# An exchange through DRAM whose four writes are cut by destination and not by source partitions

## The chip, the cores and the metric

The kernel runs on one core of a Trainium2 chip. The metric is the device time of one execution in microseconds (us), as the median of three runs; lower is better. The engines are TensorE (PE, matrix products), VectorE (DVE), ScalarE (ACT), GpSimd (POOL) and SyncE (SP, which issues transfers). SyncE, ScalarE and GpSimd each have a queue of transfers of their own (q1, q10 and q0 in the profile), and the core has 16 DMA engines that carry them out.

## The reference

There are two layers over 8 sequences of 128 tokens with 512 features, all in float32, and each adds its result to the stream. The first applies a chosen 512 x 512 matrix for each sequence and a linear layer with a low-rank mixture of two of eight experts. The second is the one around the change: attention with 32 query heads and 8 key and value heads of width 128, over a paged cache of 512 positions and the sequence's own 128 positions, and then a gated low-rank feed-forward network (16 of 64 experts).

```python
q = rope(rmsnorm(x @ Wq.T)); k = rope(rmsnorm(x @ Wk.T)); v = x @ Wv.T
k_all, v_all = concat(cache[block_table], own)     # 512 + 128 positions
scores = where(valid, q @ k_all.T * SCALE, -1e30)
o = softmax(scores) @ v_all
x = x + ffn(o @ Wo.T)
```

The valid positions of the cache come from the lengths that are given for each sequence, and those positions are below the length. Four query heads share one key and value head.

## The kernel before, in words

**The work is cut into 64 units.** A unit is one sequence and one key head with its four query heads; two units (two key heads) make a step, and four groups of two heads pass over the 8 sequences. The units run as a software pipeline that is written out by hand: every engine's order is the program's order, with no scheduler in between (`tc.manual_schedule`, L87). `iteration(u)` (L1264) computes in one pass the scores and the softmax of unit u, the product with the values of unit u - 2, the output projection of unit u - 3 and the projections and the rotary embedding of units ahead. The function runs for u from 1 to 66 (L1397); unit 0 is done beside the first layer (L732 to L828).

**The softmax of a unit.** For each of the four heads, TensorE computes 128 x 640 scores (`scores`, L434: L439 against the cache, L442 against the sequence's own keys), VectorE adds the mask and scales (`mask_exp`, L447, L452), ScalarE takes the exponential (L463), and GpSimd divides by the sum (`normalize`, L466, L469).

**The exchange.** The product with the values needs the probabilities transposed: positions on the partitions, where the softmax left tokens. The kernel does not use TensorE for that. VectorE turns the 32 x 32 blocks (`blocks`, L471, the transpose of L474), which leaves every block at its old place; moving the blocks between the partitions is done by a write to DRAM and a read back. The buffer `pb` has 128 partitions, and on each there are four stretches of 800 numbers: stretch k holds what has to get to the partitions 32 k to 32 k + 31. Of the 800, 640 are probabilities of four heads, and 160 (the rotated queries and the key of unit u + 2, turned by `blocks_qk`, L423, the transpose of L425) ride along. The units 62 and 63 have no such passengers and write 640.

- `exchange_out(u)` (L479) writes `pb` to a DRAM tile `px` of shape 4 x 32 x 4 x 800: (destination k, row b within the destination's partitions, source i, stretch). It issues four writes, two on SyncE's queue and two on ScalarE's (L486). Write i takes the partitions 32 i to 32 i + 31 with all their four stretches.
- `exchange_in(u)` (L930), called a pass later, reads it back on SyncE's queue: `qkb` (L934), then `pT` (L937), in which partition 32 k + b has its four rows of DRAM in a line.
- `heads_qk` (L940) copies `qkb` into the operand of the next unit's scores on ScalarE (L944); `values` (L950) multiplies `pT` with the values (L957).

**What orders it.** `pb` has one buffer (L421, a pool with one buffer), so the transposes of unit u + 1 into it (first L425, and then L474 four times) wait until the writes of unit u have read it. In `iteration(u)`, SyncE first issues five loads of key pages (`gather`, L182, L193), then the two reads of the exchange of unit u - 1, then three more pages (L1286 to L1290), and at the end of the pass the writes of unit u (L1372). Each of these instructions waits in its queue's order. GpSimd issues the value rows (L203, indirect), the weights (`wqkv`, `wo`) and a part of the output (`yd`, `yp`) on its own queue.

**Beside it.** The projections use products of the Strassen-Winograd kind (L243 to L284, L1079 to L1130), with the additions spread over VectorE and GpSimd. The end of the kernel has a second, smaller exchange of the same layout (`turn_out`, L377), which the change doesn't touch.

Of the kernel before, what the change touches and what calls it, by code (L numbers as in the profile page):

```python
# [33 lines left out]
QD = P // 32  # L34
# [24 lines left out]
def adaln_ffn_kernel(  # L59
# [25 lines left out]
    nc = tc.nc  # L85
# [393 lines left out]
    def exchange_out(u):  # L479

        pb = pb_t.pop(u)
        m = dram_x.tile([QD, 32, QD, XW], F32, tag="px", name=f"px_{u}")
        w = XW if u + 2 in range(4, NU) else PW
        for i in range(QD):
            eng = nc.sync if i < QD // 2 else nc.scalar
            eng.dma_start(  # L486
                out=m[:, :, i, :w].rearrange("k b f -> b k f"),
                in_=pb[i * 32 : (i + 1) * 32, :, :w],
            )
        px_t[u] = m  # L490


    with ExitStack() as l0:
# [322 lines left out]
        blocks(0, 2)  # L816
        blocks(0, 3)
        exchange_out(0)
        l0_turn(B - 2)
        l0_experts(B - 1)  # L820
# [105 lines left out]
    with ExitStack() as l1:  # L926
# [337 lines left out]
        def iteration(u):  # L1264
# [104 lines left out]
            if on(u):  # L1369
                blocks(u, REP - 2)  # L1370
                blocks(u, REP - 1)
                exchange_out(u)  # L1372
# [186 lines left out]
```

## Time and profile before

| What | Value |
|---|---|
| time, median of 3 runs | 1204.23 us (1203.33 to 1204.79) |
| profiled execution, its own time | 1207.58 us |
| its span, first to last instruction | 1205.5 us |
| granted TensorE clock | 1.0 |
| busy: ACT, POOL, DVE | 504.9, 741.0, 913.2 us |
| transfers: bytes, mean rate | 302.31 MB, 251 GB/s |
| share of 16 DMA engines: q1 (SyncE), q0 (GpSimd) | 53.1%, 12.3% |
| exchange writes, issues on SyncE / ScalarE | 128 / 128 |
| exchange reads, pT / qkb | 64 / 60 |

How to read it: the profile is of one execution, so the sums in the text are made against its own time, and the runs lie a few microseconds beside it. Busy times are unions of an engine's instructions; instructions that only issue transfers aren't counted as busy, and they stand in the timeline under the name of the queue (SPq, ACTq). The chain of waits follows the work that ended last back from the end: at each step to what released it. A line of a DMA queue has its packets, its megabytes and the time of its packets as a share of 16 engines' time in the window. A packet is what one DMA engine moves in one go; here it is a row (3200 B for an exchange write), and after the rows there are small packets of 4 B that report the end.

### The profile page before, as it was taken

To read this page: it belongs to the slowest core of one execution; us is meant where nothing else is said; L and a number is where in the kernel's file an instruction comes from. 1 tells how busy PE (TensorE), PEld (TensorE's weight loads), DVE (VectorE), ACT (ScalarE), POOL (GpSimd) and SP (SyncE) were. 2 spreads that over 40 slices of the span, in tenths; PEclk is the share of its full clock that TensorE was granted. 3 is DMA by queue.
4 is the path that set the end of the run, shared out by engine and by line. 5 is a ranking of instruction groups with operands and counts; after the bars stand their busy time and mean duration, and the time that the engine had idled before them with its cause. 6 is when DMAs were issued, how large, how long until landed. Compare 5 with 4: busy or idle time off the path is not lost.

```text
span 1205.5 us, 16789 instructions
## 1 busy us (share of the span) xinstructions
PE 1194.1 (99%) x4156; PEld 715.1 (59%) x4156; DVE 913.2 (76%) x2103; ACT 504.9 (42%) x1457; POOL 741.0 (61%) x828
## 2 busy tenths in 40 slices
PE   9999999999999999999999999999999999999998
PEld 7766555565655556555555565555656555555554
DVE  2557788788988887878887787889887788887632
ACT  1345534444444444434444444444444444443211
POOL 3554868778756777578656685787657784643100
PEclk9999999999999999999999999999999999999999
DMA  8823777888779978888889978987889888887742
GB/s 316 305 77 118 249 247 238 261 272 289 230 252 261 323 241 268 279 274 275 254 255 283 284 228 278 294 288 254 268 256 303 247 266 249 269 277 229 234 138 97
DMA packets 205444, 302.31 MB, mean 251 GB/s; under 512 B 84771, under 2 KB 119332, under 8 KB 204324
## 3 DMA queue, kind: packets, MB, share of 16 engines
q1 hardware_dynamic: 170164, 196.29, 53.1%
q10 hardware_dynamic: 18864, 52.57, 13.7%
q0 software_dynamic: 16320, 52.40, 12.3%
q8 instruction: 33, 0.54, 0.2%
q14 instruction: 63, 0.52, 0.1%
HBM read 185.44 MB, written 115.74 MB: 250 GB/s over the span
## 4 chain that ended last, share of the span: by engine, by line
PE 83%; DMA 7%; DVE 3%; POOL 2%; SPq 2%; issue 2%; ACT 1%; ACTq 0%; DVEq 0%; POOLq 0%
PE o L957 18%; PE p L262 17%; PE s L439 16%; PE y L1082 12%; PE s L442 4%; DMA kt<-in_kc 3%; PE p L295 3%; DMA px<-pb 2%; PE cp L627 2%; PE op L1446 2%; PE bp L649 2%; PE y L1095 2%; PE fr L867 1%; SPq L192 1%; DVE pb L474 1%
## 5 line engine op out<-in xcount | busy, mean ns | idle before, releaser
L463 ACT ACTIVATE p<-p,low 128x640 f32<-128x640 f32 x256 | 211.9, 828 | 429.1 <-DVE den L468 270.1
L469 POOL TENSOR_SCALAR p<-p,den 128x640 f32<-128x640 f32 x256 | 210.9, 825 | 229.8 <-DVE den L468 228.9
L452 DVE CUSTOM_DVE_ANT_0 p<-s,mask,rs 128x640 f32<-128x640 f32 x256 | 222.4, 878 | 82.2 <-PE s L442 81.3
L262 PE MATMUL p<-wqkv,xo 128*128 128x384 f32 x784 | 281.0, 487 | 0.6 <-POOL wqkv L163 0.4
L439 PE MATMUL s<-kt,qkT 128*128 128x512 f32 x504 | 258.4, 594 | 5.3 <-DMA kt<-in_kc 4.1
L957 PE MATMUL o<-pT,vt 128*128 128x512 f32 x512 | 230.2, 592 | 0.0
L474 DVE STREAM_TRANSPOSE pb<-p 128x640 f32<-128x640 f32 x248 | 204.8, 826 | 23.4 <-POOL p L469 23.2
L1082 PE MATMUL y<-wo,oT 128*128 128x256 f32 x784 | 206.5, 380 | 0.5 <-DVE yp L1151 0.4
L262 PEld LDWEIGHTS p<-wqkv,xo 128*128 128x128 f32 x784 | 148.3, 190 | 69.8 <-POOL wqkv L163 1.4
L442 PEld LDWEIGHTS s<-qkT 128*128 128x128 f32 x504 | 95.8, 190 | 120.5 <-issue 120.5
L203 POOL DMA_INDIRECT vt<-in_vc,vrow x128 | 138.2, 1080 | 41.6 <-issue 31.9
L957 PEld LDWEIGHTS o<-pT,vt 128*128 128x128 f32 x512 | 97.2, 190 | 107.9 <-issue 92.8
L439 PEld LDWEIGHTS s<-kt,qkT 128*128 128x128 f32 x504 | 94.5, 190 | 78.3 <-issue 34.5
L1082 PEld LDWEIGHTS y<-wo,oT 128*128 128x128 f32 x784 | 131.8, 191 | 9.4 <-PE s L442 0.8
L311 ACT ACTIVATE sq<-c 128x128 f32<-128x128 f32 x320 | 98.9, 309 | 9.5 <-DVE oT L474 1.4
L442 PE MATMUL s<-qkT 128*128 128x128 f32 x504 | 96.8, 274 | 0.0
L317 POOL TENSOR_TENSOR rs<-ss,mhalf 128x5 f32<-128x5 f32 x64 | 83.8, 1310 | 5.3
L980 ACT COPY oT<-o 128x512 f32<-128x512 f32 x64 | 37.5, 586 | 106.9 <-PE o L957 79.9
L315 POOL TENSOR_SCALAR ss<-ss,eps 128x5 f32<-128x5 f32 x64 | 25.0, 391 | 76.0 <-ACT sq L311 76.0
L957 PE MATMUL o<-pT,vn 128*128 128x512 f32 x128 | 65.4, 592 | 0.0
L265 DVE TENSOR_TENSOR c<-c,p 128x384 f32<-128x384 f32 x84 | 44.9, 534 | 25.6 <-PE p L262 25.5
L425 DVE STREAM_TRANSPOSE pb<-ca 128x640 f32<-128x640 f32 x60 | 50.1, 834 | 17.2 <-DMA kt<-in_kc 11.7
(198 smaller groups left out, 1442.5 us busy)
## 6 DMA issues: line engine op xcount, KB each, us to landing
pT<-px SPq DMA_DIRECT2D x64, 1280.0 KB
px<-pb SPq DMA_DIRECT2D x120, 400.0 KB
px<-pb ACTq DMA_DIRECT2D x120, 400.0 KB
qkb<-px SPq DMA_DIRECT2D x60, 320.0 KB
kt<-in_kc SPq DMA_DIRECT2D x512, 32.0 KB
wqkv<-in_wqkv POOLq DMA_DIRECT2D x32, 384.0 KB, 4.6
wo<-in_wo POOLq DMA_DIRECT2D x17, 512.0 KB, 7.8
yd<-yp POOLq DMA_DIRECT2D x12, 512.0 KB, 9.3
```

What stands on the lines that cost most here:

```text
L203: nc.gpsimd.indirect_dma_start(out=kv_t[step][1][:, c, :], out_offset=None, in_=vc, in_offset=bass.IndirectOffsetOnAxis(ap=vrow[:, hf, at ...
L262: nc.tensor.matmul(out=ps, lhsT=xo[:, pr, x, c, :], rhs=w[:, c, :], start=(c == 0), stop=(c == 1))
L311: nc.scalar.activation(sq, cs[:, at : at + D], AF.Square, accum_out=ss[:, h : h + 1])
L317: nc.gpsimd.tensor_tensor(rs, ss, mhalf, ALU.pow)
L439: nc.tensor.matmul(out=s[:, :L], lhsT=qkT[:, h, :], rhs=kt[:, :, g % GH, :], start=True, stop=True)
L442: nc.tensor.matmul(out=s[:, L:NK], lhsT=qkT[:, h, :], rhs=qkT[:, REP, :], start=True, stop=True)
L452: nc.vector.tensor_tensor_reduce(out=p, in0=s_t.pop((u, h))[:, :NK], in1=mask_t[st], scale=rs_t[u][:, h : h + 1], scalar=BIG, op0=ALU.add, ...
L463: nc.scalar.activation(p, p, AF.Exp, bias=low, scale=-1.0, accum_out=den)
L469: nc.gpsimd.tensor_scalar(p_t[u, h], p_t[u, h], den, 1.0, ALU.mult, ALU.mult)
L474: nc.vector.transpose(pb_t[u][:, :, h * w : (h + 1) * w].rearrange("p i (j a) -> p j i a", a=32), p_t.pop((u, h)).rearrange("p (j i a) -> ...
L957: nc.tensor.matmul(out=o, lhsT=vt[:, c, j * D : (j + 1) * D] if c < LC else vn_t.pop(u), rhs=pT[:, c], start=(c == 0), stop=(c == LC),)
L1082: nc.tensor.matmul(out=y_t["y"][:, half * HN : (half + 1) * HN], lhsT=part(key)[:, i * S : (i + 1) * S], rhs=wo_t[:, slot(w, key[0] // (B ...
```

## The change

Before, write i takes 32 partitions and serves all four destinations; after it, write k takes one stretch from all 128 partitions and serves one destination. The number of writes, the queues, the bytes and the places in DRAM stay the same, and so do the two reads. In `exchange_out` (L479):

```diff
-        for i in range(QD):
-            eng = nc.sync if i < QD // 2 else nc.scalar
+        for k in range(QD):
+            eng = nc.sync if k < QD // 2 else nc.scalar
             eng.dma_start(
-                out=m[:, :, i, :w].rearrange("k b f -> b k f"),
-                in_=pb[i * 32 : (i + 1) * 32, :, :w],
+                out=m[k, :, :, :w].rearrange("b i f -> i b f"),
+                in_=pb[:, k, :w],
             )
```

As the instructions carry it, a write before goes over its target as 32 x 4 x 800 numbers and over its source as 32 x 4 x 800 (32 partitions, four stretches). After the change the target is gone over as 4 x 32 x 800 (source block i outermost, then the row b), and the source as 128 x 800. A run of 800 numbers is 3200 B in both, and there are 128 of them in each write. The orders of the instructions on TensorE, VectorE and GpSimd are the same in both kernels; on SyncE and ScalarE only these writes differ.

## Prediction

> **What bounds the kernel now.** I read the page from its chain of waits, then SyncE's timeline of one unit, then the queues and packets of the exchange. The shares and the chain:
>
> ```profile
> PE 1194.1 (99%) x4156; PEld 715.1 (59%) x4156; DVE 913.2 (76%) x2103; ACT 504.9 (42%) x1457; POOL 741.0 (61%) x828
> ...
> PE 83%; DMA 7%; DVE 3%; POOL 2%; SPq 2%; issue 2%; ACT 1%; ACTq 0%; DVEq 0%; POOLq 0%
> PE o L957 18%; PE p L262 17%; PE s L439 16%; PE y L1082 12%; PE s L442 4%; DMA kt<-in_kc 3%; PE p L295 3%; DMA px<-pb 2%; PE cp L627 2%; PE op L1446 2%; PE bp L649 2%; PE y L1095 2%; PE fr L867 1%; SPq L192 1%; DVE pb L474 1%
> ```
>
> TensorE sets the end (83% of the chain), but transfers hold 7% of it, and the exchange's writes 2% (2.4% in the chain in order of time, 29 us). So the exchange is nearly late already. One unit on SyncE's queue:
>
> ```profile
> 335.26 0.81 SPq L486 DMA_DIRECT2D px<-pb  x2
> 337.48 6.23 SPq L193 DMA_DIRECT2D kt<-in_kc  x5
> 343.89 0.54 SPq L934 DMA_DIRECT2D qkb<-px  x1
> 344.48 0.62 SPq L937 DMA_DIRECT2D pT<-px  x1
> 345.62 2.02 SPq L193 DMA_DIRECT2D kt<-in_kc  x3
> 351.67 0.81 SPq L486 DMA_DIRECT2D px<-pb  x2
> ```
>
> This is a closed loop. The read qkb waits for all four writes. The one buffer pb is refilled by the VectorE transpose of L425 (343.94 here) only once they have left it, and then come four transposes of L474 and the next four writes at 351.67: 16.4 us a turn. Over the turns in the packet records: 7.9 us (median) from the issue to the write's last packet (0.8 until the first, 7.1 of packets), then 8.5 us to the next issue, 7.0 in the shortest turn. The writes follow one another strictly; what a write lasts longer, beyond what TensorE's own work covers, lengthens every turn. From exchange 2 (issued at 142.9) to exchange 63 (1136.9) there are 61 turns.
>
> **What the change keeps.** Four writes a unit, two on SyncE and two on ScalarE; 128 rows of 3200 B each, the same bytes, places and waits. No instruction of TensorE, VectorE or GpSimd moves. Only the walk differs: the target was walked 32 x 4 x 800 and is now walked 4 x 32 x 800, while the source is 128 rows instead of 32 x 4. So two things can change: how many of the 16 DMA engines share one write, and what one packet lasts.
>
> **How many engines.** Each engine that works on a transfer ends its share with a 4-byte packet. ScalarE's queue shows it:
>
> ```profile
> q10 hardware_dynamic: 18864, 52.57, 13.7%
> ```
>
> It carried 131 transfers (128 exchange writes, one xT, two wqkv), and 131 x (128 + 16) = 18864: 128 rows and 16 small packets each. In the packet records q1 has 13618 packets of 4 B for 853 transfers: 851 x 16, plus two with one each. Those two are ids and pg, which have a single row. In the first 2.5 us q1 shows only ids, with a data packet and one small packet:
>
> ```profile
> q1 hardware_dynamic: 2, 0.00, 0.0%
> ...
> ids<-in_lora_ids SPq DMA_DIRECT2D x1, 0.0 KB
> ```
>
> So a first count of 1 uses one engine, first counts of 32 and 128 use 16. No row has 4. The bounds are 1 engine and 16; I take **4**, the reading that both rows fit: a transfer is dealt out along its first count, at most to 16. I also take it that every write gets the same four, so that 12 stand idle; no row shows which engines a smaller transfer gets, and four different fours would be the 16-engine rival again. The step to 4 is an inference from two far rows, and the largest risk here.
>
> [...]
>
> **What a packet lasts.** In windows with only this exchange, the first with SyncE's first write alone, the second with both queues' writes:
>
> ```profile
> q1 hardware_dynamic: 29, 0.09, 94.1%
> ```
> ```profile
> q1 hardware_dynamic: 47, 0.15, 53.6%
> q10 hardware_dynamic: 48, 0.15, 47.8%
> ```
>
> The last column is a share of 16 engines: 0.941 x 16 x 0.5 us / 29 = 260 ns; then 0.536 x 16 x 0.8 / 47 = 146 ns and 0.478 x 16 x 0.8 / 48 = 127 ns. Over the whole execution the 3200 B packets average 189 ns on SyncE's queue and 160 on ScalarE's, with a floor of 126. Bounds 126 and 260; I take 175, the mean of the two averages, since four engines with two queues each are neither the crowd of the first row nor surely the order of the second.
>
> [...]
>
> **The sum.** Each of the four engines gets 4 x 128 / 4 = 128 packets a unit (32 before): 128 x 0.175 = 22.4 us. Other transfers share these engines: GpSimd's queue 12.3% of 1205.5 us, 2.3 us for each of 64 units, and kt 1.1 us (8 transfers of 128 packets of 18 ns over 16 engines); 2.7 of these 3.4 fall into a window that is three quarters of the turn. 22.4 + 2.7 = 25.1 us of packets against 7.1: +18.0 a turn. The 8.5 us after a landing may shrink towards 7.0, as TensorE has run ahead by then (VectorE's own work between 343.94 and 351.67 is 6.9 us): bounds 0 to -1.5, I take -0.75. So **+17.2 us a turn**, 33.6 in all.
>
> Does that turn hold the rest? The four engines need 22.4 + 3.4 + 4.3 (reads qkb and pT: 32 packets of 32 ns and 32 of 102 each) = 30.1 of 33.6. TensorE's 16.4 us of a unit fit as well. ScalarE's and SyncE's issues (0.36 and 0.33 us each) could grow to the 0.54 of the qkb row: at most 0.4 us a turn. kt's issues queue behind the write on SyncE, where the next instruction waits for that write anyway. A long write could also hold its issuing engine; no row shows that, and I put 0 to 2 us on it and take 0.
>
> 61 x 17.2 = 1049. At the ends: exchange 2 waits on SyncE for exchange 1 (+10), and the last unit's L957 waits longer for pT: write and read take some 31 us where 21 lie between now (1136.9 to 1157.8), and I take half of the 10 as hidden behind the gate work there (+5). 1207.6 (the profiled execution; its span is 1205.5) + 1049 + 15 = 2272; the median of the runs shown lies 3.4 lower: **2268 us**.
>
> **Rivals.**
> - *Four engines, packets at the floor.* 128 x 0.126 + 2.7 = 18.8; +11.7 - 0.75 = 11.0; 61 x 11.0 + 15 gives 1890; with -1.5 about 1840. For it: with a quarter of the engines, the memory side has room. Against it: the floor held only while the two queues read different partitions.
> - *Four engines that meet.* 128 x 0.260 + 2.7 = 36.0; +28.9 - 0.75 = 28.1; 61 x 28.1 + 15 gives 2935. For it: 32 packets at 260 ns whenever one write runs alone; both queues now walk the same rows. Against it: in the second window the engines fell out of step by themselves.
> - *All 16 engines stay* (the other side). If the shares are dealt by rows, whatever their order, a write takes every partition and no packet lasts 260 ns: 32 x 0.126 + 1.1 = 5.1 us instead of 7.1. TensorE fills 99% of the span, so only what the chain holds for px is to be won: 29 us x 2.0 / 7.9 = 7, 1197 us; down to 1180 if kt's waits shorten with it. It decides only where all 16 engines take part: with 8, 64 x 0.126 + 1.1 = 9.2 us is still over 7.1.
> - *One engine.* 512 x 0.126 = 64.5 us: 61 x 59.4 + 15 gives about 4840. Only the row of ids speaks for it, and that had nothing to divide.
>
> **Chances.** Forecast (2050 to 2600) 0.50; floor (below 2050) 0.20; meeting (above 2600) 0.18; 16 engines 0.10; one engine 0.02. The range from the floor to the meeting case, 1830 to 2935, leaves out about 0.15. A measurement of this kernel can tell about 0.2% from no change. The 16-engine case is faster in 0.06, the same in 0.02, slower in 0.02; all else is slower: 0.92.
>
> **What would show it.** Right: q10 at 17328 packets (131 x 144 less 128 x 12); the DMA row near 4 tenths instead of 8, TensorE near 53%; SyncE from px to qkb 26 us, from qkb to px about 7.5; the chain mostly "DMA px<-pb", and VectorE waiting at L425. Wrong step by step: 18864 packets refute the four engines; 17328 with px to qkb near 20 or 37 us refutes the 175 ns; a much longer stretch from qkb to px shows a held engine that I left at nothing.

## The result and the profile after

The changed kernel takes 2070.57 us (median of 6 runs, 2064.45 to 2075.05) against 1203.78 us for the kernel before in the same runs: a ratio of 1.7192, with a 95% interval of 1.7158 to 1.7226. The profiled execution's span is 2072.0 us, against 1205.5. The forecast was 2268 us with a range of 1830 to 2935.

The page of the changed kernel, in its shares, its DMA row (tenths of 16 engines, in 40 slices) and its chain of waits:

```profile
PE 1365.2 (66%) x4156; PEld 786.9 (38%) x4156; DVE 911.6 (44%) x2103; ACT 503.8 (24%) x1457; POOL 736.6 (36%) x828
...
DMA  8334444444354344444435334444444444454343
...
DMA 62%; PE 11%; issue 10%; DVE 9%; POOL 4%; ACT 2%; SPq 1%; ACTq 0%; DVEq 0%; POOLq 0%
DMA px<-pb 58%; DVE pb L474 5%; POOL p L469 3%; PE o L957 2%; PE cp L627 1%; PE op L1446 1%; PE bp L649 1%; PE p L262 1%; DMA pT<-px 1%; DMA kt<-in_kc 1%; DVE yp L1151 1%; PE s L439 1%; DVE c L265 1%; PE p L295 1%; DMA px<-wo 1%
```

The chain has turned over: 83% TensorE before, now 58% one transfer, the exchange's write. At the same time the 16 DMA engines are busy in 4 tenths instead of 8. The bottleneck is DMA, and the DMA row is half empty: such a pair suggests that the work isn't spread over the engines.

The packets of ScalarE's queue say how far it is spread (packets, MB, share of 16 engines):

```profile
q10 hardware_dynamic: 17328, 52.56, 7.8%
```

That is 1536 fewer than the 18864 before: 128 writes times 12. Each write ends in 4 small packets instead of 16. The packet records agree: in 94% of the time in which rows of an exchange write are under way, there are at most four of them, from both queues together, where 16 was the commonest number before. So both queues share the same four engines. The share of 7.8% looks harmless; on four engines it is four times as much.

One turn on SyncE's queue of the changed kernel (start, duration):

```profile
701.70 1.21 SPq L486 DMA_DIRECT2D px<-pb  x2
704.29 8.33 SPq L193 DMA_DIRECT2D kt<-in_kc  x5
723.82 0.59 SPq L934 DMA_DIRECT2D qkb<-px  x1
724.46 0.61 SPq L937 DMA_DIRECT2D pT<-px  x1
725.60 2.03 SPq L193 DMA_DIRECT2D kt<-in_kc  x3
730.70 2.15 SPq L486 DMA_DIRECT2D px<-pb  x2
```

From the write's issue to the read 22.1 us, where it was 8.6; from the read to the next write 6.9, where it was 7.8. VectorE shows who waits in between. The first two lines are its timeline, the third is from the list of waits (sum in us, times, longest), and the last is that wait in the kernel before, from the list of those who waited for px (sum, times):

```profile
710.52 0.16 DVE L468 RECIPROCAL den<-den 128x1 f32<-128x1 f32 x1
723.96 0.84 DVE L425 STREAM_TRANSPOSE pb<-ca 128x640 f32<-128x640 f32 x1 [13.29 <-DMA px<-pb]
```
```profile
DVE pb L425 <- DMA px<-pb: 810.6, 58, 18.2
```
```profile
  DVE pb L425: 5.0, 6
```

The refill of pb stood 13.3 us for the write of the unit before. Over the execution this wait alone is 810.6 us (5.0 before), and the span grew by 866.5. Between exchanges 2 and 63 lie 61 turns in both traces: 993.7 us before (142.9 to 1136.6), 1836.7 after (159.6 to 1996.3). That is 843.0 of the growth; the way to exchange 2 took 16.7 longer, what follows exchange 63 took 6.8.

### The profile page after: what moved, and what is told of

The parts are those of the page before. It is cut to its first block, busy times and chain, and to the rows that moved or that the text cites. A ratio compares the mean times of both kernels' runs of the same rounds, so it can differ in the third digit from the quotient of the medians.

```text
span 2072.0 us, 16791 instructions
## 1 busy us (share of the span) xinstructions
PE 1365.2 (66%) x4156; PEld 786.9 (38%) x4156; DVE 911.6 (44%) x2103; ACT 503.8 (24%) x1457; POOL 736.6 (36%) x828
## 3 DMA queue, kind: packets, MB, share of 16 engines
q10 hardware_dynamic: 17328, 52.56, 7.8%
## 4 chain that ended last, share of the span: by engine, by line
DMA 62%; PE 11%; issue 10%; DVE 9%; POOL 4%; ACT 2%; SPq 1%; ACTq 0%; DVEq 0%; POOLq 0%
DMA px<-pb 58%; DVE pb L474 5%; POOL p L469 3%; PE o L957 2%; PE cp L627 1%; PE op L1446 1%; PE bp L649 1%; PE p L262 1%; DMA pT<-px 1%; DMA kt<-in_kc 1%; DVE yp L1151 1%; PE s L439 1%; DVE c L265 1%; PE p L295 1%; DMA px<-wo 1%
## 5 line engine op out<-in xcount | busy, mean ns | idle before, releaser
L262 PE MATMUL p<-wqkv,xo 128*128 128x384 f32 x784 | 327.7, 545 | 361.6 <-DVE c L265 354.7
L439 PE MATMUL s<-kt,qkT 128*128 128x512 f32 x504 | 306.1, 693 | 311.8 <-ACT qkT L944 285.8
L425 DVE STREAM_TRANSPOSE pb<-ca 128x640 f32<-128x640 f32 x60 | 50.7, 845 | 828.4 <-DMA px<-pb 810.6
L957 PE MATMUL o<-pT,vt 128*128 128x512 f32 x512 | 256.6, 648 | 5.1 <-DMA pT<-px 5.1
L439 PEld LDWEIGHTS s<-kt,qkT 128*128 128x128 f32 x504 | 106.9, 221 | 398.6 <-ACT qkT L944 310.6
L1082 PE MATMUL y<-wo,oT 128*128 128x256 f32 x784 | 234.7, 421 | 6.5 <-DVE yp L1151 4.6
L957 PEld LDWEIGHTS o<-pT,vt 128*128 128x128 f32 x512 | 111.8, 219 | 138.6 <-issue 130.7
L442 PEld LDWEIGHTS s<-qkT 128*128 128x128 f32 x504 | 108.5, 215 | 146.8 <-issue 146.8
L1082 PEld LDWEIGHTS y<-wo,oT 128*128 128x128 f32 x784 | 146.9, 212 | 25.6 <-PE s L442 5.3
L1151 DVE TENSOR_TENSOR yp<-yp,y 128x512 f32<-128x512 f32 (+3 forms) x94 | 59.9, 637 | 0.0
L311 ACT ACTIVATION_READ_ACCUMULATOR sq<-c 128x1 f32 x320 | 59.8, 187 | 0.0
```

What stands on the lines that cost most here:

```text
L262: nc.tensor.matmul(out=ps, lhsT=xo[:, pr, x, c, :], rhs=w[:, c, :], start=(c == 0), stop=(c == 1))
L311: nc.scalar.activation(sq, cs[:, at : at + D], AF.Square, accum_out=ss[:, h : h + 1])
L439: nc.tensor.matmul(out=s[:, :L], lhsT=qkT[:, h, :], rhs=kt[:, :, g % GH, :], start=True, stop=True)
L442: nc.tensor.matmul(out=s[:, L:NK], lhsT=qkT[:, h, :], rhs=qkT[:, REP, :], start=True, stop=True)
L957: nc.tensor.matmul(out=o, lhsT=vt[:, c, j * D : (j + 1) * D] if c < LC else vn_t.pop(u), rhs=pT[:, c], start=(c == 0), stop=(c == LC),)
L1082: nc.tensor.matmul(out=y_t["y"][:, half * HN : (half + 1) * HN], lhsT=part(key)[:, i * S : (i + 1) * S], rhs=wo_t[:, slot(w, key[0] // (B ...
```

## The experiments

In the packet records, a turn can be cut in three: from the first issue to the first packet, the time from the first to the last packet of the write, and from there to the next issue. All numbers are means over the turns 2 to 61, in us, and the packet is a row of 3200 B. The first count, of which the expectations speak, is the outermost of the counts by which a write goes over its target or its source (the smaller one, where the two differ):

```
kernel       DMA engines    turn   to first   packets   to next   ns per   time, us
             for a write            packet              issue     packet   (ratio to before)
before       16             16.28     0.88       7.08     8.32     174.6   1203.78
after         4             30.21     1.23      21.58     7.40     146.5   2070.57 (1.72)
two_counts    2             45.06     1.21      36.36     7.49     135.7   3017.72
one_queue     4             29.81     1.27      21.12     7.42     145.5   2053.33
far_rows      4             29.80     1.20      21.20     7.39     145.2   2044.47
sixteen      16             18.24     1.62       8.60     8.02     160.5   1332.89 (1.11)
rows         16             18.95     2.29       6.51    10.15     133.2   1370.95 (1.14)
crossed      16             17.22     0.96       8.59     7.67     222.7   1262.33 (1.05)
```

The kernel before ran beside each of the experiments, at medians of 1205.55 to 1206.12 us. two_counts, one_queue, far_rows, before_pool and three_one were run once, the others 4 to 10 times.

### Half the first count: two_counts

```diff
+            for i in (0, 2):
                 eng.dma_start(
-                    out=m[k, :, :, :w].rearrange("b i f -> i b f"),
-                    in_=pb[:, k, :w],
+                    out=m[k, :, i : i + 2, :w].rearrange("b i f -> i b f"),
+                    in_=pb[i * 32 : (i + 2) * 32, k, :w],
                 )
```

> Each of the four writes by destination is cut in two, so that its target is walked 2 x 32 x 800 and its source has 64 partitions; eight writes a unit, same rows, places and bytes. Theory (a write is dealt out along its first count, always over the same lowest engines): two engines get 256 packets each a unit. With the 146 ns a packet that the changed kernel shows, 256 x 0.1465 + 2.8 = 40.3 us of packets instead of 21.6; a turn of 30.2 + 18.7 = 48.9; 2071 + 61 x 18.7 = 3210 us, 2890 at the floor of 126 ns. q10 shows 256 x 66 + 432 = 17328 packets. Rival (a small transfer gets other engines each time, or the number does not come from the first count): the eight writes spread, the time is 2071 or less, and the packets on q10 are another number (17840 with four engines each).

Measured: 3017.72 us and 17328 packets on q10.

```profile
q10 hardware_dynamic: 17328, 52.56, 4.8%
```

The theory's number of packets comes out, and the time lies between its floor (2890) and its value (3210). The write's packets take 36.4 us, against 21.6 with four engines; from about the sixteenth microsecond on, 16 packets end in a microsecond (2 engines / 0.126 us = 15.9), where four engines reach 31.7. So the number of engines follows the first count, and the eight writes don't spread over others: in 95% of the time in which rows are under way, there are at most two. That all writes share the same engines was an assumption of the prediction, and this run supports it; which of the 16 they are, the records don't tell, so "lowest" in the theory is not shown. The miss within the theory is the packet: 136 ns on average instead of the 146.5 that I had carried over.

### One queue: one_queue

```diff
-            eng = nc.sync if k < QD // 2 else nc.scalar
+            eng = nc.sync
```

> The changed kernel with all four writes on SyncE's queue. Theory (the four engines' own rate bounds a write, whatever queue it comes from): 128 packets an engine as before, so 2071 within 60 us; q10 shows only 432 packets. Rival (the two queues disturb each other on the four engines, or their descriptors come late because of each other): without the second queue the slow first 4 us of each write go, about 3 us a turn, and the time falls to 1890 or so. Second rival (one queue alone can't keep four engines full): above 2200.

Measured: 2053.33 us, and on the queue of ScalarE only what it loads itself:

```profile
q10 hardware_dynamic: 432, 0.79, 0.1%
```

One queue fills the four engines as well as two do. Both rivals fall: the packets take 21.1 us instead of 21.6.

### The same cut on 16 engines: sixteen and rows

In sixteen each write by destination is split into its four sources, so that its first count is 32 again:

```diff
+            for i in range(QD):
                 eng.dma_start(
-                    out=m[k, :, :, :w].rearrange("b i f -> i b f"),
-                    in_=pb[:, k, :w],
+                    out=m[k, :, i, :w],
+                    in_=pb[i * 32 : (i + 1) * 32, k, :w],
                 )
```

> The same cut by destination and the same places, but each write is split into its four sources: 16 writes a unit of 32 partitions x 800, eight on each queue, source by source within a destination. First count 32, so 16 engines by the theory. Packets as in the kernel before (7 us of packets a unit); added are 12 issues a unit of 0.33 to 0.52 us, six on each queue (2 to 3 us until the last one is out), and a semaphore's turn comes round after eight transfers. Theory: 1204 + 61 x (1 to 5) = 1265 to 1510 us, and q10 shows 64 x 8 x 48 + 432 = 25008 packets. Rival (the order by destination itself, or where its rows fall in DRAM, costs the time): stays near 2071.

Measured: 1332.89 us, ratio 1.1081 (1.1020 to 1.1141), and 25008 packets on q10, as worked out. The order by destination and the places in DRAM are those of the changed kernel, so neither is what costs 867 us.

```profile
q10 hardware_dynamic: 25008, 52.59, 13.0%
```

What is left of the loss, 127 us, goes with the 16 issues; no run separates them from the rest. On ScalarE's timeline the eight issues stretch over 7.9 us, and its next copy stands behind them:

```profile
710.73 7.88 ACTq L487 DMA_DIRECT2D px<-pb  x8
718.65 0.59 ACT L981 COPY oT<-o 128x512 f32<-128x512 f32 x1 [7.86 <-DMA px<-pb]
```

In rows there are four writes from all 128 partitions, and the DRAM tile is laid out so that a write is one line; the reads are cut into four for it:

```diff
-        m = dram_x.tile([QD, 32, QD, XW], F32, tag="px", name=f"px_{u}")
+        m = dram_x.tile([QD, QD, 32, XW], F32, tag="px", name=f"px_{u}")
...
-                out=m[k, :, :, :w].rearrange("b i f -> i b f"),
+                out=m[k, :, :, :w].rearrange("i b f -> (i b) f"),
...
-            nc.sync.dma_start(out=pT, in_=m[:, :, :PW])
+            for k in range(QD):
+                nc.sync.dma_start(
+                    out=pT[k * 32 : (k + 1) * 32],
+                    in_=m[k, :, :, :PW].rearrange("i b f -> b i f"),
+                )
```

(and the same four reads for qkb).

> Four writes by destination, each from all 128 partitions, but the DRAM tile is laid out as destination, source, row: a write is 128 x 800 in one line on both sides. The reads pay for it: qkb and pT are read in four parts each, 32 partitions from 32 x 4 runs. Theory: 16 engines for writes (q10 back at 18864 packets) and reads; a write of all partitions takes 5 to 7 us of packets instead of 21.6; the eight reads cost six more issues of about 0.55 us on SyncE, 3.3 us a turn, partly hidden: 1190 to 1400 us. Rival (the rows' order by destination is what costs): near 2071.

Measured: 1370.95 us, ratio 1.1383 (1.1363 to 1.1403). Its queue and a turn on SyncE:

```profile
q10 hardware_dynamic: 18864, 52.57, 10.3%
```
```profile
706.04 1.79 SPq L935 DMA_DIRECT2D qkb<-px  x4
708.23 1.81 SPq L942 DMA_DIRECT2D pT<-px  x4
710.56 2.06 SPq L193 DMA_DIRECT2D kt<-in_kc  x3
714.42 4.79 SPq L486 DMA_DIRECT2D px<-pb  x2
```

18864 packets: with a first count of 128 on both sides, all 16 engines work (131 x 144 packets, 16 small ones a write). This is the cut by destination without the loss of engines. Its rows last 133 ns on average, against 175 before; the wish to read from all partitions has something to it. But the packets of a unit take only 0.6 us less (6.51 against 7.08), because SyncE's two issues now lie 4.5 us apart in this turn (4.79 us for the pair, 0.81 before; 4.35 apart on average). The list of waits of SyncE's queue shows what the second one stands for:

```profile
SPq L486 <- DMA px<-pb: 228.4, 56, 7.3
```

In the records of the instructions, the transfers of SyncE and ScalarE share eight semaphores in rotation (123 transfers on each in the kernel before), and an issue names its own semaphore as one that it waits for, that is, for the landing of the transfer that had it last. With six reads more in the rotation, SyncE's second write comes upon the semaphore of a write that ScalarE has just issued for the same exchange (58 of 62 times), so it is issued when that one has landed (here at 718.88, 0.02 us after it). The stretch from the last packet to the next issue, in which the cut reads lie, grew too, from 8.3 to 10.2 us.

### Which partitions run together: crossed

```diff
-            eng = nc.sync if i < QD // 2 else nc.scalar
+            eng = nc.sync if i % 2 == 0 else nc.scalar
```

This is an edit of the kernel before.

> The kernel before (writes by source, 16 engines) with the two queues' shares exchanged: SyncE issues sources 0 and 2, ScalarE 1 and 3, so that the two writes in flight together take partitions 0 to 31 and 32 to 63, then 64 to 95 and 96 to 127, where before they took 0 to 31 beside 64 to 95. Nothing else changes. Theory (packets last about 250 ns where the engines meet on the same quarter-pairs of partitions, 126 ns where they don't): most packets at 220 to 260 ns, 8.5 to 9.5 us of packets a unit instead of 7.1, +1.4 to 2.4 us a turn, of which some may be hidden: 1240 to 1345 us. Rival (a packet's length depends on how many transfers run, not on which partitions): mean packet within 10 ns of 175, time within 6 us of 1204.

Measured: 1262.33 us, ratio 1.0463 (1.0422 to 1.0503). The rows last 209 ns on SyncE's queue and 237 on ScalarE's (189 and 160 before), and the share of ScalarE's queue shows it at once, with the packets unchanged:

```profile
q10 hardware_dynamic: 18864, 52.57, 19.2%
```

(13.7% before.) The theory holds: 53% of the rows last 220 to 260 ns (15% before), and the packets of a unit take 8.6 us instead of 7.1. So a row's duration went with which partitions the two queues read at the same time (222.7 ns on average against 174.6), and the kernel before had the better of these two pairings already. One thing else differs: rows written at the same time lie 3200 instead of 6400 B apart in DRAM. before_far, below, moves them far apart without effect at the old pairing; the crossed pairing was not run that way.

### Other fours: pool_queue, before_pool and three_one

```diff
-            eng = nc.sync if k < QD // 2 else nc.scalar
+            eng = nc.gpsimd
```

> The changed kernel with all four writes on GpSimd's queue, whose transfers are dealt out by another generator. The walk, the rows and the first count of 4 stay. Theory (it is the same four engines for all four writes that costs; other fours for each write would not): if this queue gives each write another four, each engine gets 32 packets a unit, 7 to 8 us of packets, and four issues of about 1.1 us each (the indirect loads on this queue take 1.08) come upon GpSimd: 1215 to 1400 us. [...] Rival (a write on four engines is slow by itself, wherever they are, or this queue gives the same four as well): 1900 to 2200 us.

> The control to the run above: the kernel before, writes by source (first count 32), all four on GpSimd's queue. It prices the move to that queue: four issues of about 1.1 us a unit on an engine that is 61% busy, 4.3 of 16.4 us. Both theories: 1215 to 1330 us. If this is as slow as the run above, the four writes of the run above cost nothing more than the queue.

Measured: 1939.43 us for pool_queue (1.6072, 1.5992 to 1.6152), 1377.41 for before_pool, the same line in the kernel before. The theory's 1215 to 1400 us is missed by far, and the time lies in the rival's 1900 to 2200. before_pool is above its 1215 to 1330 as well, with a turn of 19.1 us; why was not followed up. But it is 562 us faster than pool_queue, so the cut by destination costs on this queue too. The page of the kernel before lists this queue as q0 software_dynamic and the other two as hardware_dynamic; how it chooses its engines, no record tells. Two things happened in pool_queue. First, the fours do differ: while the writes run, the records show most often 4, 8 or 12 of their packets under way at once, which four engines could not hold. Second, GpSimd did not get the fourth write out: it is issued 9.4 us after the first on average, as in this stretch of its timeline (9.25 us):

```profile
970.10 2.18 POOL L486 DMA_DIRECT2D px<-pb  x3
979.35 0.69 POOL L486 DMA_DIRECT2D px<-pb  x1 [7.07 <-issue]
```

In before_pool the four follow each other within 1.8 us. Therefore the next run sends three writes by GpSimd's queue and one by SyncE's:

```diff
-            eng = nc.sync if k < QD // 2 else nc.scalar
+            eng = nc.gpsimd if k < QD - 1 else nc.sync
```

> The changed kernel with three writes on GpSimd's queue and the fourth on SyncE's. With all four on GpSimd's the records show 8 and 12 packets under way at once, so the writes did get different fours, but the fourth was issued 9.4 us after the first. Here none is issued late. Theory (four engines for a write cost because all four writes share them): the writes of a unit run beside each other on up to 16 engines, 32 packets of 3200 B each an engine; at 126 to 250 ns and with 2.8 us of others and the slow start of some 3 us, 10 to 14 us of packets a unit instead of 21.6; a turn of 19 to 24 us, 1400 to 1720 us. Rival (a write on four engines is slow in itself): 1900 us or more.

Measured: 1838.91 us, a turn of 26.5, with the last write issued 3.4 us after the first on average. This lies between the theory's 1720 and the rival's 1900 and misses as well: other engines for each write are not enough. GpSimd's packets (two rows, 6400 B) have a median of 244 ns but a mean of 534, since half of the first 24 of a unit take over a microsecond. In the first two microseconds some 10 to 13 rows end in each, with pool_queue's several fours as with one four:

```
rows (3200 B) ended in each us from the write's first packet, mean over the turns
us            1     2     3     4     5     6     7     8    10    14    18
before      59.2 101.8 103.3  89.0  88.5  46.2  17.8   5.4    -     -     -
rows        66.1 123.3 117.4  62.9  53.6  54.4  24.4   7.5    -     -     -
after       11.5  10.4  10.8  21.6  24.6  26.9  27.2  26.2  22.7  29.9  31.2
one_queue   11.4  10.6  13.6  21.2  27.0  29.4  26.0  24.9  22.4  30.9  31.4
far_rows    12.3  13.2  13.3  21.6  24.5  26.4  26.2  25.3  22.4  29.8  31.5
two_counts   6.7   6.8   8.0  11.1  13.3  13.8  12.5  10.7  11.7  15.2  16.2
pool_queue  10.4   9.9  20.3  34.2  37.4  39.7  39.8  31.8  51.4  23.6   5.0
```

The engines are not idle in that time: in the changed kernel 3.3 of the 4 possible rows are under way on average, and each lasts long (333 ns). If a write is dealt out along its first count of 4, each engine gets 32 partitions in a line, and all its engines start at the first of their 32, in every write. They may wait for each other there until they have fallen out of step; crossed shows that rows got longer by which partitions were read together (222.7 ns against 174.6), but the records don't name the partition of a packet, so this is not shown.

### The slow start: far_rows and before_far

The other thing that the four engines would do in step, dealt out like this, is writing rows of DRAM that lie side by side (3200 B apart). Here the tile is laid out with the source outermost:

```diff
-        m = dram_x.tile([QD, 32, QD, XW], F32, tag="px", name=f"px_{u}")
+        m = dram_x.tile([QD, QD, 32, XW], F32, tag="px", name=f"px_{u}")
...
-                out=m[k, :, :, :w].rearrange("b i f -> i b f"),
+                out=m[:, k, :, :w],
...
-            m = px_t.pop(u).rearrange("k b i f -> (k b) i f")
+            m = px_t.pop(u).rearrange("i k b f -> (k b) i f")
```

> The changed kernel with the DRAM tile laid out as source, destination, row: the same four writes, each walked 4 x 32 x 800 with a first count of 4, but the four engines of a write now fill four places that lie 409600 B apart, where they lay 3200 B apart. The reads stay one each. It is for the slow start of each write (in its first 4 us some 12 packets end in a us, later 32). Theory (the slow start comes from where the four engines read, partitions 0, 32, 64, 96 in step): 2071 within 25 us. Rival (it comes from four engines writing neighbouring rows of DRAM in step): 2 to 3 us a turn go, 1890 to 1950 us.

> The kernel before with that same DRAM layout (source, destination, row); writes by source, first count 32, 16 engines. Theory (the layout costs nothing): 1204 within 6 us. Rival (neighbouring rows in DRAM slow the writes): the 7.1 us of packets a unit shorten by up to 1 us, and 1175 to 1198 us.

Measured: 2044.47 us for far_rows in one run, just outside the 25 us of the theory and far from the rival's 1950; its start is as slow (12 to 13 rows a microsecond). That the rows lie side by side is not the reason. before_far takes 1203.61 us against 1206.12 beside it, ratio 0.9981 (0.9972 to 0.9991): as forecast within 6 us, and if anything faster by 0.1 to 0.3%. It is the only version here that isn't slower than the kernel before, and its gain is at the edge of what can be measured.

## Why the prediction was right, step by step

**The loop.** Right. The writes follow one another, pb's refill at L425 is the place where the loss shows (810.6 of 866.5 us), and 61 turns carry 843.0 of the growth. The expected profile came: "the chain mostly DMA px<-pb", the DMA row at 4 tenths, 17328 packets.

**Four engines.** Right. It was an inference from transfers with first counts of 1, 32 and 128; the rows under way at once (at most four in 94% of the time, and at most two in 95% in two_counts) show it, and sixteen and rows show that a first count of 32 or 128 brings back 16 engines with the same cut. The small packets agree in each: 4 a write in the changed kernel and 2 in two_counts (17328 packets on q10 in both), 16 in sixteen (25008) and in rows (18864).

**What a packet lasts: the term that was mis-sized.** The prediction put 175 ns, "the mean of the two averages" of the kernel before. Measured are 146.5: 128 x 0.1465 = 18.8 us a turn instead of 22.4. That mean belonged to a crowd of 16 engines. Here neither bound alone holds: the upper one, 260, is passed with 333 ns in the first 2 us of a write, and the lower one is reached with 126 to 128 from the thirteenth microsecond on. A row's duration was not one number but a course. The prediction's own sign says the same: SyncE's way from px to qkb takes 23.3 us on average, between the forecast 26 and the 20 that was to refute the 175 ns. The rest of the turn: 2.8 us of other transfers and gaps (21.58 - 18.75; forecast 2.7), 1.2 us to the first packet (0.8), 7.4 us after the last (8.5 less 0.75; the mean before was 8.3). Together 30.2 instead of 33.6. 61 x 3.4 = 207 us too much in the turns, less 8.5 too little at the ends (23.5 instead of 15), is about the 197 us by which the forecast of 2268 missed. The chosen 175 was a mean of two numbers and not a reading of four engines; that 2268 came within 10% is in part luck.

**The two rivals on four engines** framed it: the floor would have been 1890, the meeting 2935. The rows begin as long as in the second, or longer, and end as in the first.

**The 16-engine rival** didn't occur as a whole, but rows shows its premise: rows last 133 ns when 16 engines read all partitions. Its gain of 2.0 us a unit would have come out at 0.6 there, with issues 4.5 us apart.

**Issues.** I bounded them at 0.54 us each; SyncE's and ScalarE's now have medians of 0.61, a little over the bound, and 0.52 (0.33 and 0.41 before). They cost little, as expected: SPq and ACTq hold 1% and 0% of the chain. "A long write could also hold its issuing engine", put at 0 to 2 us and taken as 0: the stretch from the last packet to the next issue did not get longer (7.4 us).

**TensorE's share** was forecast at 53% and is 66%. With the busy time of before, the shorter span would have made it 58% (1194.1 / 2072.0); the rest is that the same products were busy for 1365.2 us, since the clock fell (below).

**What stays open** is why the first three microseconds of such a write run at a third of the rate. It is neither the second queue nor the neighbouring rows in DRAM: one_queue ends 11.4 rows in the first microsecond and far_rows 12.3, where the changed kernel ends 11.5. That the engines start on partitions that get in each other's way is argued from crossed and not shown: no kernel here lets the four start elsewhere.

## What to carry to other kernels

On the queues of SyncE and ScalarE, a write's first count decided over how many DMA engines it was dealt out (2, 4 and 16 engines for first counts of 2, 4 and 32 or 128, by the small packets), and an innocent rearrangement that puts 4 in front of 32 left 12 of 16 without a part in it; count the small packets in the queue line before believing a share. Rows, bytes and issues may all be the same: a chain of waits full of DMA above a half-empty DMA row is a sign to look for. And before an exchange is recut so that its writes get better, the reads have to be priced: in rows the writes did, and the kernel still lost 14%.

## What the runs showed of the hardware that was not expected

**The granted TensorE clock was lower in the runs in which TensorE idled more.** It was 1.000 before, 0.814 after (TensorE busy in 66% of the span), 0.719 in two_counts (46%), 0.852 in three_one (74%), 0.955 in rows (91%) and 0.996 in crossed (96%). After a wait of 10.5 us the first two products take 2.08 us, twice the 1.02 of later ones; TensorE's timeline of the changed kernel, with the idle time before in brackets, and the same two products for another head, 8.2 us later:

```profile
700.26 2.08 PE L439 MATMUL s<-kt,qkT 128*128 128x512 f32 x2 [10.46 <-ACT qkT L944]
...
708.43 1.02 PE L439 MATMUL s<-kt,qkT 128*128 128x512 f32 x2
```

The granted clock is 0.50 from the restart at 700.3 until 705.6 and 1.00 after it, so here the full rate is back 5.4 us after the restart. It can have cost the change little, since TensorE holds only 11% of the chain; I read the slower clock here as an effect of the stall and not as its cause.

**The other pairing cost 4.6%.** That two writes of 32 partitions slow each other or not, by which 32 they are (222.7 ns a row in crossed, 174.6 before), is worth 56 us on this kernel, without a packet more.
